# Expert layers that compute each token's own experts only, in four layers of cross-attention and mixture of experts

## The chip, the cores and the metric

The kernel runs on one core of one Trainium2 chip. Its time is the device time of one execution in microseconds. A time of a kernel is the median of its runs; a profile belongs to one execution, whose own time is given beside it. TensorE is called PE (its weight loads PEld), VectorE DVE, ScalarE ACT, GpSimd POOL, SyncE SP.

## The reference

The input x is 8 batches of 128 tokens of 128 channels, in fp32, and there is a context of the same shape. Four layers each add an attention and then a feed-forward of experts:

```python
x = x + L0_xattn(layernorm(x), ctx)     # talking heads
x = x + L0_ffn(layernorm(x))
x = x + L1_xattn(layernorm(x), ...)     # an mLSTM
x = x + L1_ffn(layernorm(x), ...)       # holds one more attention and a layer norm of its own
x = x + L2_xattn(layernorm(x), ...)
x = x + L2_ffn(layernorm(x), ...)
x = x + L3_xattn(ctx, layernorm(x), ...)
x = x + L3_ffn(layernorm(x), ...)
```

In each feed-forward a router gives every token one score for each of 8 experts. Layer 0 takes the best two of 8 experts (hidden width 176, silu gate) with the softmax of the two scores as weights. Layer 1 takes the best one of 8 (width 512, gelu, weight 1). Layer 2 takes the best two of 8 (width 256, silu gate, sigmoid scores divided by their sum) and adds a shared expert. Layer 3 has 7 experts (width 512, silu gate) and 8 router columns; it takes the best one with twice its softmax probability, none where the eighth column wins, and adds a shared expert:

```python
for j in range(NUM_EXPERTS - 1):
    mask = (ind == j)[..., None]
    acc = acc + swiglu(x, Wu[j], Wg[j], Wd[j]) * mask
out = out + ALPHA * p * acc
out = out + swiglu(x, Wu_s, Wg_s, Wd_s)
```

The reference computes every expert on every token and masks. What a token gets is only the output of its own experts.

## The kernel before

The 8 tiles of x (128 tokens by 128 channels) stay in SBUF. Tokens are worked on in two halves of 4 batches, 512 columns each. The stages follow one another, and each engine takes its instructions in a fixed order, which follows the order of the program closely: attention 0 (the L0 talking heads), experts f0, the mLSTM (stage name L1 attention), attention m1 (inside layer 1's feed-forward), experts f1, attention m2, experts f2, attention m3, experts f3.

`layernorm` takes half of the tokens: bn_stats and bn_aggr for each batch on DVE, the power -0.5 for four batches at once on POOL (L108), then z for each batch on DVE. `transposed` turns z into channels by tokens with four PE transposes. `router_logits`, `rank`, `share` and `chosen` give for each half a gate for every token and expert, zero for those not chosen.

`experts` is dense: for each unit (an expert, or in f0 two experts packed together) it loads the weights `w` on SP's queue (L206, four buffers, so loads run ahead), and for each half and each 128 wide chunk of hidden channels computes g (L213) and u (L220) as matmuls of 128x512, silu on ACT (L225) or gelu (L217), and their product on DVE (L226). The down matmuls y (L231) have 128 columns for a batch. DVE adds y times the gate to x (L241, L243).

`attention` (m1, m2, m3) goes over the 8 batches as a software pipeline. In each round DVE takes the negative maxima of the next batch's scores (nmp, L318); `outputs` of the batch before makes the attention's values av (L357), their reciprocal sums rd (L363), cT (L365), the output projection with wo and calls `finish`, which adds to x (`add_to_x` L383, or `to_x1` at L728 and L729); then `weights` transposes the maxima (nt, L330), adds them to q (qm, L332), and makes st and its exponentials pt (L345):

```python
for b in range(B + 1):
    if b + 1 < B:
        q0s[b + 1] = maxima(b + 1, *halves[(b + 1) // HB])
    if b > 0:
        outputs(b - 1, pts.pop(b - 1))
    if b < B:
        pts[b] = weights(b, q0s.pop(b), halves[b // HB][1])
```

PSUM is shared by two tags: `mm` with 6 banks for wide results and `o` with 2 banks. `vz` is a large zeroed tile that POOL fills ahead of the mLSTM (L538). At the end SP stores the 8 tiles of x.

Of the kernel before, what the change touches and what calls it, by code (L numbers as in the profile page):

```python
# [8 lines left out]

FP = mybir.dt.float32  # L10
U8 = mybir.dt.uint8
AF = mybir.ActivationFunctionType
# [20 lines left out]
C_N = 612  # L33
# [16 lines left out]
def blocks(ctx: ExitStack, tc: tile.TileContext, t: dict, out: bass.AP):  # L50
# [3 lines left out]
    act = ctx.enter_context(tc.tile_pool(name="act", bufs=1))  # L54
    small = ctx.enter_context(tc.tile_pool(name="small", bufs=3))
    wpool = ctx.enter_context(tc.tile_pool(name="wpool", bufs=4))
# [24 lines left out]
    ones = keep.tile([1, P], FP, name="ones")  # L81
    nc.gpsimd.memset(ones, 1.0)
# [9 lines left out]
    low = cst[:, C_LOW : C_LOW + 64]  # L92
# [5 lines left out]
    def layernorm(src, name):  # L98
# [10 lines left out]
        z = act.tile([P, HB, P], FP, name=f"z_{name}", tag="z", bufs=3)  # L109
# [20 lines left out]
    def router_logits(zT, wcol, brow, name):  # L130
        lg = bank_o(f"lg_{name}")
        for j in range(HB):
            dst = lg[:, j * E : (j + 1) * E]
            nc.tensor.matmul(
                dst, lhsT=zT[:, j * P : (j + 1) * P], rhs=wsm[:, wcol : wcol + E],
                start=True, stop=brow is None,
            )
            if brow is not None:
                nc.tensor.matmul(
                    dst, lhsT=ones, rhs=row[:, brow : brow + E], start=False, stop=True  # L140
                )
        v = small.tile([P, HB, E], FP, name=f"v_{name}", tag="rt_v")
        nc.vector.tensor_copy(v.rearrange("p b e -> p (b e)"), lg[:, : HB * E])
        return v

    def over_experts(v, op, name, negate=False):
        m = small.tile([P, HB], FP, name=f"m_{name}", tag=f"rt_m{op}")
        nc.vector.tensor_reduce(m, v, AX.X, op, negate=negate)
        return m

    def spread(m):
        return m.unsqueeze(2).to_broadcast([P, HB, E])

    def rank(v, name):

        full = [P, HB, E, E]
        of_j = v.unsqueeze(2).to_broadcast(full)
        of_e = v.unsqueeze(3).to_broadcast(full)
        gt = small.tile(full, FP, name=f"gt_{name}", tag="rt_gt", bufs=2)
        eq = small.tile(full, FP, name=f"eq_{name}", tag="rt_eq", bufs=2)  # L160
        nc.vector.tensor_tensor(gt, of_j, of_e, ALU.is_gt)
        nc.vector.tensor_tensor(eq, of_j, of_e, ALU.is_equal)
        eqf = eq.rearrange("p b e j -> p b (e j)")
        gtf = gt.rearrange("p b e j -> p b (e j)")
        nc.vector.tensor_tensor(
            eqf, eqf, low.unsqueeze(1).to_broadcast([P, HB, E * E]), ALU.mult
        )
        nc.vector.tensor_tensor(gtf, gtf, eqf, ALU.add)
        rk = small.tile([P, HB, E], FP, name=f"rk_{name}", tag="rt_rk")
        nc.vector.tensor_reduce(rk, gt, AX.X, ALU.add)  # L170
        return rk

    def softmax_terms(v, name):
        nm = over_experts(v, ALU.max, f"max_{name}")
        d = small.tile([P, HB, E], FP, name=f"d_{name}", tag="rt_d")
        nc.vector.tensor_tensor(d, v, spread(nm), ALU.subtract)
        e = small.tile([P, HB, E], FP, name=f"e_{name}", tag="rt_e")
        nc.scalar.activation(e, d, AF.Exp)
        return e

    def share(v, name):

        s = over_experts(v, ALU.add, f"sum_{name}")
        r = small.tile([P, HB], FP, name=f"r_{name}", tag="rt_r")
        nc.vector.reciprocal(r, s)
        g = small.tile([P, HB, E], FP, name=f"g_{name}", tag="rt_g")
        nc.vector.tensor_tensor(g, v, spread(r), ALU.mult)
        return g

    def chosen(rk, n, v, name):  # L190
        c = small.tile([P, HB, E], FP, name=f"c_{name}", tag="rt_c")
        if v is None:
            nc.vector.tensor_scalar(c, rk, float(n), None, ALU.is_lt)
        else:
            nc.vector.scalar_tensor_tensor(c, rk, float(n), v, ALU.is_lt, ALU.mult)
        return c

    def experts(name, wdram, cols, zT, gates, func, nchunk, gated, down):

        with tc.tile_pool(name=f"h_{name}", bufs=2) as hidp:
            for u in range(wdram.shape[0]):
                w = wpool.tile([P, cols], FP, name=f"w_{name}_{u}", tag="w")
                nc.sync.dma_start(out=w, in_=wdram[u])  # L206
                up0 = nchunk * P
                dn0 = 2 * nchunk * P if gated else nchunk * P
                for hf in range(NH):
                    hid = hidp.tile([P, nchunk, HT], FP, name=f"hid_{name}_{u}_{hf}", tag="hid")  # L210
                    for c in range(nchunk):
                        g = bank_mm(f"g_{name}_{u}_{hf}_{c}")
                        nc.tensor.matmul(  # L213
                            g, lhsT=w[:, c * P : (c + 1) * P], rhs=zT[hf], start=True, stop=True
                        )
                        if not gated:
                            nc.scalar.activation(hid[:, c, :], g, func)  # L217
                            continue
                        up = bank_mm(f"u_{name}_{u}_{hf}_{c}")
                        nc.tensor.matmul(  # L220
                            up, lhsT=w[:, up0 + c * P : up0 + (c + 1) * P], rhs=zT[hf],
                            start=True, stop=True,
                        )
                        sg = hidp.tile([P, HT], FP, name=f"sg_{name}_{u}_{hf}_{c}", tag="sg", bufs=3)
                        nc.scalar.activation(sg, g, func)  # L225
                        nc.vector.tensor_tensor(hid[:, c, :], up, sg, ALU.mult)  # L226
                    for col, parts in down(u):
                        y = bank_o(f"y_{name}_{u}_{hf}_{col}")
                        for j in range(HB):
                            for n, (c, r0, k) in enumerate(parts):  # L230
                                nc.tensor.matmul(  # L231
                                    y[:, j * P : (j + 1) * P],
                                    lhsT=hid[r0 : r0 + k, c, j * P : (j + 1) * P],
                                    rhs=w[r0 : r0 + k, dn0 + c * P : dn0 + (c + 1) * P],
                                    start=n == 0, stop=n == len(parts) - 1,
                                )
                        for j in range(HB):
                            xb = x[hf * HB + j]
                            yj = y[:, j * P : (j + 1) * P]
                            if col is None:  # L240
                                nc.vector.tensor_tensor(xb, yj, xb, ALU.add)  # L241
                            else:
                                nc.vector.scalar_tensor_tensor(  # L243
                                    xb, yj, gates[hf][:, j, col : col + 1], xb, ALU.mult, ALU.add
                                )
# [144 lines left out]

    with tc.tile_pool(name="a0", bufs=2) as ap:
        w0 = ap.tile([P, 4, 1024], FP, name="w0", bufs=1)
        for i in range(4):
            nc.sync.dma_start(out=w0[:, i, :], in_=t["w0"][:, i, :])
        th = ap.tile([P, 2, 16], FP, name="th", bufs=1)
# [10 lines left out]
        for hf in range(NH):  # L408
# [81 lines left out]
            def outputs(j, pr):  # L490
# [35 lines left out]
                add_to_x(b, o[:, :P])  # L526


            prs = [weights(0)]
            for j in range(HB):  # L530
                if j + 1 < HB:
                    prs.append(weights(j + 1))
                outputs(j, prs[j])

# [13 lines left out]
    )  # L548


    zTs, gates = [], []
    for hf in range(NH):
        zT = transposed(layernorm(half(hf), f"f0_{hf}"), f"f0_{hf}")
        v = router_logits(zT, W_G0, None, f"f0_{hf}")
        rk = rank(v, f"f0_{hf}")
        gates.append(share(chosen(rk, 2, softmax_terms(v, f"f0_{hf}"), f"f0_{hf}"), f"f0_{hf}"))
        zTs.append(zT)
    experts(
        "f0", t["f0"], 9 * P, zTs, gates, AF.Silu, 3, True,
        lambda u: [  # L560
            (2 * u, [(0, 0, P), (2, 0, M0_REST)]),
            (2 * u + 1, [(1, 0, P), (2, 64, M0_REST)]),
        ],
    )


# [153 lines left out]
    for hf in range(NH):  # L720
        z = layernorm(half(hf), f"f1_{hf}")
        z1 = layernorm([z[:, j, :] for j in range(HB)], f"f1i_{hf}")
        zTs.append(transposed(z1, f"f1i_{hf}", W_LN))
        for j in range(HB):
            nc.gpsimd.tensor_copy(x1[hf * HB + j], z[:, j, :])

    def to_x1(b, o):
        nc.vector.tensor_tensor(x1[b], o, x1[b], ALU.add)  # L728
        nc.gpsimd.tensor_tensor(x[b], x[b], x1[b], ALU.add)  # L729
# [188 lines left out]
```

## Time and profile before

| what | value |
|---|---|
| median of 3 runs | 1165.52 us (1152.72, 1165.52, 1170.35) |
| profiled execution | 1148.92 us, span 1147.1 us, mean granted PE clock 0.891 |
| PE busy | 998.9 us (87%) |
| DVE, ACT, POOL busy | 487.6, 312.9, 137.8 us |
| DMA | 23.27 MB, mean 20 GB/s |
| stage attention 0 | 0 to 237 us |
| stages f0; f1; f2; f3 | 237 to 347; 547 to 669; 764 to 866; 960 to 1147 us |
| stages mLSTM; m1; m2; m3 | 347 to 452; 452 to 547; 669 to 764; 866 to 960 us |

The stage bounds are read from the timeline, rounded, so that windows can be cut there. The profile gives for each group of instructions the source line, the engine, the operation, the tiles written and read (out<-in), the shapes, the count, the busy time and the mean duration, then the idle time of the engine ahead of it and what ended most of that idle time. A row of the windows gives start and end, length, busy time and number of instructions for PE, PEld, DVE, ACT and POOL, the granted PE clock, the share of DMA time and GB/s. A row of the timeline gives the start, the time from the first to the last of a run of like instructions, engine, line, operation and tiles, and in brackets an idle time before it with its releaser.

### The profile page before, as it was taken

To read this page: it belongs to the slowest core of one execution; us is meant where nothing else is said; L and a number is where in the kernel's file an instruction comes from. 1 tells how busy PE (TensorE), PEld (TensorE's weight loads), DVE (VectorE), ACT (ScalarE), POOL (GpSimd) and SP (SyncE) were. 2 spreads that over 40 slices of the span, in tenths; PEclk is the share of its full clock that TensorE was granted. 3 is DMA by queue.
4 is the path that set the end of the run, shared out by engine and by line. 5 is a ranking of instruction groups with operands and counts; after the bars stand their busy time and mean duration, and the time that the engine had idled before them with its cause. 6 is when DMAs were issued, how large, how long until landed. Compare 5 with 4: busy or idle time off the path is not lost.

```text
span 1147.1 us, 15509 instructions
## 1 busy us (share of the span) xinstructions
PE 998.9 (87%) x6356; PEld 650.3 (57%) x6356; DVE 487.6 (43%) x1226; ACT 312.9 (27%) x691; POOL 137.8 (12%) x151
## 2 busy tenths in 40 slices
PE   5877977879997992888899988879997887999998
PEld 2456645755556452565677745646664665666665
DVE  3344434443342546564311144644446463433333
ACT  1445345431111111222233311223221222322221
POOL 0112012220002212330000032200004120000000
PEclk9799979989995865889899988989998786999999
DMA  6000000000001000000010000000111000001000
GB/s 246 1 1 1 1 1 1 1 5 19 18 19 37 1 0 0 1 2 1 19 37 33 28 15 1 1 1 29 42 56 55 1 2 1 28 28 35 22 1 19
DMA packets 8892, 23.27 MB, mean 20 GB/s; under 512 B 1010, under 2 KB 4212, under 8 KB 8692
## 3 DMA queue, kind: packets, MB, share of 16 engines
q1 hardware_dynamic: 8098, 20.06, 5.2%
q10 hardware_dynamic: 722, 2.21, 0.5%
q8 instruction: 50, 0.82, 0.3%
q14 instruction: 22, 0.18, 0.1%
HBM read 21.74 MB, written 0.52 MB: 19 GB/s over the span
## 4 chain that ended last, share of the span: by engine, by line
PE 67%; issue 14%; DVE 12%; ACT 3%; POOL 2%; DMA 1%; POOLq 0%; DVEq 0%; SPq 0%; ACTq 0%
PE y_f L231 11%; PE u_f L220 10%; PE g_f L213 10%; DVE nmp L318 4%; PE mx L248 4%; PE st_m L248 3%; PE sc_m L248 3%; PE m L248 2%; PE av_m L357 2%; PE qk L248 2%; PE gb L248 2%; PE av L248 2%; PE st L461 1%; PE kp_m L280 1%; PE o L522 1%
## 5 line engine op out<-in xcount | busy, mean ns | idle before, releaser
L231 PEld LDWEIGHTS y_f<-w_f,hid_f 128*128 128x128 f32 (+1 forms) x1472 | 186.0, 192 | 68.0 <-issue 31.0
L231 PE MATMUL y_f<-w_f,hid_f 128*128 128x128 f32 (+1 forms) x1472 | 202.2, 284 | 1.0 <-DVE hid_f L226 1.0
L225 ACT ACTIVATE sg_f<-g_f 128x512 f32<-128x512 f32 x124 | 74.0, 597 | 262.2 <-PE g_f L213 169.0
L220 PE MATMUL u_f<-zT_f,w_f 128*128 128x512 f32 x248 | 133.2, 620 | 0.0
L213 PE MATMUL g_f<-zT_f,w_f 128*128 128x512 f32 x248 | 133.2, 620 | 0.0
L226 DVE TENSOR_TENSOR hid_f<-u_f,sg_f 128x512 f32<-128x512 f32 x124 | 85.4, 689 | 86.8 <-PE u_f L220 83.3
L345 ACT ACTIVATE pt_m<-st_m 128x512 f32<-128x512 f32 x96 | 50.2, 602 | 168.7 <-PE st_m L248 168.1
L243 DVE SCALAR_TENSOR_TENSOR x<-y_f,c_f,x 128x128 f32<-128x128 f32 x120 | 33.8, 344 | 140.1 <-PE y_f L231 140.1
L248 PE MATMUL st_m<-qm_m,kT_m 32*128 32x256 f32 x384 | 48.1, 470 | 31.7 <-DVE qm_m L332 31.7
L318 DVE TENSOR_REDUCE nmp<-sc_m 128x4 f32<-128x512 f32 x96 | 59.4, 685 | 34.3 <-PE sc_m L248 34.3
L220 PEld LDWEIGHTS u_f<-zT_f,w_f 128*128 128x128 f32 x248 | 45.9, 199 | 44.0 <-issue 43.2
L213 PEld LDWEIGHTS g_f<-zT_f,w_f 128*128 128x128 f32 x248 | 46.0, 201 | 39.7 <-issue 38.9
L248 PE MATMUL mx<-s,kron 128*128 128x512 f32 x64 | 43.8, 772 | 25.1 <-DVE s L469 13.9
L243 DVE SCALAR_TENSOR_TENSOR x<-y_f,g_f,x 128x128 f32<-128x128 f32 x128 | 36.0, 344 | 66.3 <-PE y_f L231 66.3
L213 PE MATMUL g_f<-zT_f1e,w_f 128*128 128x512 f32 x128 | 63.3, 616 | 0.0
L248 PE MATMUL sc_m<-km_m,qT_m 32*128 32x256 f32 x384 | 58.7, 478 | 1.0 <-DVE nmp L318 0.6
L217 ACT ACTIVATE hid_f<-g_f 128x512 f32<-128x512 f32 x64 | 38.2, 597 | 74.2 <-PE g_f L213 74.2
L484 POOL TENSOR_TENSOR pr<-pr,rs 128x512 f32<-128x512 f32 x32 | 33.2, 1039 | 163.6 <-DVE rs L483 134.5
L248 PEld LDWEIGHTS st_m<-qm_m,kT_m 32*128 32x128 f32 x384 | 25.9, 207 | 41.4 <-DVE qm_m L332 37.6
L477 ACT ACTIVATE pr<-mx,nm 128x128 f32<-128x128 f32 x128 | 45.3, 369 | 12.4 <-DVE nm L474 12.4
L248 PEld LDWEIGHTS sc_m<-km_m,qT_m 32*128 32x128 f32 x384 | 40.0, 220 | 14.3 <-ACT pt_m L345 7.0
L108 POOL TENSOR_TENSOR rs_a<-ve_a,nhalf 128x4 f32<-128x4 f32 x8 | 8.1, 1014 | 328.2 <-DVE ve_a L106 328.2
(207 smaller groups left out, 1283.5 us busy)
## 6 DMA issues: line engine op xcount, KB each, us to landing
w_f<-in_f SPq DMA_DIRECT2D x8, 768.0 KB, 4.2
w_f<-in_f SPq DMA_DIRECT2D x8, 512.0 KB, 3.4
w_f<-in_f SPq DMA_DIRECT2D x9, 384.0 KB, 2.9
w_f<-in_f SPq DMA_DIRECT2D x4, 576.0 KB, 8.3
w<-in_w SPq DMA_DIRECT2D x4, 512.0 KB, 8.4
wsm<-in_wsm ACTq DMA_DIRECT2D x1, 1194.0 KB, 7.8
x<-in_x SPq DMA_DIRECT2D x8, 64.0 KB, 3.5
ctxT<-in_ctxT ACTq DMA_DIRECT2D x1, 512.0 KB, 4.5
```

Of the source, the lines that this page charges most:

```text
L213: nc.tensor.matmul(g, lhsT=w[:, c * P : (c + 1) * P], rhs=zT[hf], start=True, stop=True)
L217: nc.scalar.activation(hid[:, c, :], g, func)
L220: nc.tensor.matmul(up, lhsT=w[:, up0 + c * P : up0 + (c + 1) * P], rhs=zT[hf], start=True, stop=True,)
L225: nc.scalar.activation(sg, g, func)
L226: nc.vector.tensor_tensor(hid[:, c, :], up, sg, ALU.mult)
L231: nc.tensor.matmul(y[:, j * P : (j + 1) * P], lhsT=hid[r0 : r0 + k, c, j * P : (j + 1) * P], rhs=w[r0 : r0 + k, dn0 + c * P : dn0 + (c + 1 ...
L243: nc.vector.scalar_tensor_tensor(xb, yj, gates[hf][:, j, col : col + 1], xb, ALU.mult, ALU.add)
L248: nc.tensor.matmul(dst, lhsT=w, rhs=src, start=True, stop=True)
L318: nc.vector.tensor_reduce(nmp[:, :, r * 32 + 8 : r * 32 + 153 : 144], sc[r].rearrange("p (c h k) -> p c h k", c=2, h=2), AX.X, ALU.max, ne ...
L345: nc.scalar.activation(pt[:, r].rearrange("p c h q -> p (c h q)"), st[r], AF.Exp)
L477: nc.scalar.activation(pr[:, gg, :], m3[:, g, :], AF.Exp, bias=nm[:, g : g + 1], accum_out=sums[:, gg : gg + 1],)
L484: nc.gpsimd.tensor_tensor(pr[:, part, :], pr[:, part, :], rs.unsqueeze(2).to_broadcast([P, 4, P]), ALU.mult,)
```

## The change

The dense loops are gone. Each expert layer is now an object of the class `Routed` with these steps.

- `route(b, src)` is called once for each batch, from the attention's `finish`: a layer norm of one batch (with the power on POOL), one PE transpose, logits, the best values and their indices (DVE max and max_index), one-hot rows, and a matmul with a triangle of ones that counts at which position of its expert's region each token stands; then POOL scatters the rows of z, once for each chosen expert, to `routed_z` in DRAM by an indirect DMA. A region holds 1024 rows for each expert.
- `run` computes a fixed number of blocks of 128 rows. The first 128 rows of each expert are the static groups, up to four experts together; their weights are loaded ahead (`static_weights`, tag ws). After them `table` makes, on PE and DVE, a list of what further blocks there are. Up to 15 (f0, f2) or 7 (f1, f3) further blocks come in groups of four: SP reads a word of the table into a register and uses it as the address of the weight load and of the row load; the results are stored on SP at the same address in `routed_y`. The weight buffers for these are 8 in f0 and 4 in f1 to f3.
- `combine` gathers each token's results from `routed_y` by an indirect DMA on POOL and adds them to x with the gate.

The shared experts of f2 and f3 are dense as before (`shared`). Blocks computed are the same number whatever the tokens chose. At the start SP fills `routed_z` and `routed_y` with zeros (10240 rows of 512 bytes each). SP issues 197 transfers in place of 51, reads 44 words into registers, and POOL issues 96 indirect transfers. In f0 each expert has weights of its own, 320 KB, where two shared a unit of 576 KB.

The core of the diff:

```diff
+        def route(self, b, src):
+            z = layernorm1(src, name)
+            pb = bank_o(f"rt_{name}")
+            nc.tensor.transpose(pb[:, :P], z, ident)
+            zT = self.zT[:, b * P : (b + 1) * P]
...
+            nc.tensor.matmul(lg, lhsT=zT, rhs=wsm[:, self.wcol : self.wcol + E], ...)
...
+                nc.vector.tensor_copy(v, lg)
+            nc.vector.max(out=vm, in_=v)
+            nc.vector.max_index(out=ix, in_max=vm, in_values=v)
+            nc.vector.tensor_tensor(oh, ..., iota8..., ALU.is_equal)
...
+            nc.tensor.matmul(pos, lhsT=tri, rhs=c, start=True, stop=False)
+            nc.tensor.matmul(pos, lhsT=ones128, rhs=self.sums, start=False, stop=True)
+            nc.vector.tensor_tensor(sums, self.sums, c, ALU.add)
+            nc.vector.tensor_tensor(sel, oh, pos..., ALU.mult)
+                nc.vector.tensor_reduce(self.idx[:, b, :], sel, AX.X, ALU.add)
+            for k in range(top):
+                nc.gpsimd.indirect_dma_start(
+                    out=self.views[b * top + k],
+                    out_offset=bass.IndirectOffsetOnAxis(ap=self.idx[:, b, k : k + 1], axis=0),
+                    in_=z, in_offset=None,
+                )
...
+                for q in range(2):
...
+                    load = nc.sync.dma_start(out=zq[:, :m, :], in_=by_expert(routed_z)[:, es, :])
+                    yq = blocks_of(zq, static[es], m, f"{name}_{q}")
+                    nc.scalar.dma_start(out=by_expert(yv[q])[:, es, :], in_=yq[:, :m, :])
+                tab = self.table()
+                for i0 in range(0, n, 4):
...
+                            r = nc.values_load(tab[0:1, i : i + 1], engines=[mybir.EngineType.SP], ...)
+                            nc.sync.dma_start(
+                                out=w, in_=wdram[bass.ds(r // B, 1)].rearrange("o p c -> p (o c)")
+                            )
+                            nc.sync.dma_start(
+                                out=zq[:, i - i0, :],
+                                in_=by_block(routed_z)[bass.ds(r, 1)].rearrange("o p c -> p (o c)"),
+                            )
...
+                    yq = blocks_of(zq, ws, m, f"{name}_d{i0}")
+                    for i in range(m):
+                        nc.sync.dma_start(out=by_block(yv[2 + i0 + i])[bass.ds(at[i], 1)]..., in_=yq[:, i, :])
...
+        def combine(self, b, gates):
+            for k in range(self.top):
+                nc.gpsimd.indirect_dma_start(
+                    out=yk, out_offset=None, in_=routed_y,
+                    in_offset=bass.IndirectOffsetOnAxis(ap=self.idx[:, b, k : k + 1], axis=0),
+                )
+                    nc.vector.scalar_tensor_tensor(
+                        x[b], yk, gates[:, b, k : k + 1], x[b], ALU.mult, ALU.add
+                    )
...
+        for dram in (routed_z, routed_y):
+            nc.sync.dma_start(
+                out=dram.rearrange("(p n) c -> p n c", n=BLOCKS),
+                in_=zero.unsqueeze(1).to_broadcast([P, BLOCKS, P]),
+            )
...
                 add_to_x(b, o[:, :P])
+                f0.route(b, x[b])
...
+    wst = ctx.enter_context(tc.tile_pool(name="wst", bufs=9))
+    wdyn = ctx.enter_context(tc.tile_pool(name="wdyn", bufs=4))
+    ws1 = static_weights(wst, "f1", t["f1"], 8 * P, 0, E)
...
     def to_x1(b, o):
         nc.vector.tensor_tensor(x1[b], o, x1[b], ALU.add)
         nc.gpsimd.tensor_tensor(x[b], x[b], x1[b], ALU.add)
+        f1.route(b, x1[b])
...
-    experts(
-        "f1", t["f1"], 8 * P, zTs, gates, AF.Gelu_apprx_tanh, 4, False,
-        lambda u: [(u, every4)],
-    )
+    f1.run(t["f1"], 8 * P, ws1, hidden_plain, parts_of(4, 4), wdyn)
+    for b in range(B):
+        f1.combine(b, None)
...
+    shared("f2s", ws2[E], f2.zT, 2)
+    f2.run(t["f2"], 6 * P, ws2[:E], hidden_gated(2), parts_of(2, 4), wdyn)
```

`blocks_of` transposes the four blocks of rows into one PSUM bank (PE), copies them to SBUF (DVE), computes the hidden part (`hidden0`, `hidden_plain` or `hidden_gated`: PE matmuls of 128 columns, the activation on ACT over up to 512 columns, the product on DVE), the down matmuls into one bank, and copies the results out on ACT.

More of the change, by code (lines that the diff above doesn't have):

```diff
@@ L190, in chosen @@
[L190 to L210, printed above, removed]
+            v = self.v[:, b, :]
```

491 lines of the change are left out of this document (336 added, 155 removed).

## The prediction

> **What bounds the kernel now.** I read, in this order: the page's engine rows and clock, the chain that ended last, the groups of the expert loops, the table of windows by stage, and the timeline of one batch of an attention.
>
> ```profile
> span 1147.1 us, 15509 instructions
> PE 998.9 (87%) x6356; PEld 650.3 (57%) x6356; DVE 487.6 (43%) x1226; ACT 312.9 (27%) x691; POOL 137.8 (12%) x151
> ...
> PE 67%; issue 14%; DVE 12%; ACT 3%; POOL 2%; DMA 1%; POOLq 0%; DVEq 0%; SPq 0%; ACTq 0%
> ...
> L231 PE MATMUL y_f<-w_f,hid_f 128*128 128x128 f32 (+1 forms) x1472 | 202.2, 284 | 1.0 <-DVE hid_f L226 1.0
> ...
> L220 PE MATMUL u_f<-zT_f,w_f 128*128 128x512 f32 x248 | 133.2, 620 | 0.0
> ```
>
> PE is busy 87% and two thirds of the last chain: the kernel as a whole is PE-bound. But it has two kinds of stages. Windows (length, then busy time of PE, PEld, DVE, ACT, POOL with counts, granted clock, DMA share, GB/s), here layer 0's experts, attention 1, experts 1, experts 2, experts 3:
>
> ```profile
> 237.00:347.00 110.00, 102.72 (x375) 59.33 (x374) 45.63 (x131) 19.22 (x30) 7.51 (x6) 0.90 0.05 16
> ...
> 452.00:547.00 95.00, 74.89 (x874) 51.97 (x872) 52.75 (x120) 20.54 (x37) 24.35 (x32) 0.84 0.01 1
> 547.00:669.00 122.00, 119.67 (x664) 86.71 (x664) 24.70 (x89) 39.62 (x66) 3.68 (x6) 0.96 0.08 28
> ...
> 764.00:866.00 102.00, 98.53 (x446) 61.47 (x447) 47.61 (x133) 25.79 (x41) 1.16 (x1) 0.97 0.13 43
> ...
> 960.00:1147.10 187.10, 178.61 (x864) 113.11 (x858) 69.72 (x164) 45.78 (x75) 1.01 (x1) 0.97 0.06 20
> ```
>
> Expert stages are PE and nothing else (clock 0.90 to 0.97). The attentions are not: a batch there is a round of waits, 7.8 us from one nmp to the next (514.99 to 522.76):
>
> ```profile
> 514.99 2.48 DVE L318 TENSOR_REDUCE nmp<-sc_m 128x4 f32<-128x512 f32 x4 [0.32 <-PE sc_m L248]
> 517.44 0.96 DVE L363 RECIPROCAL rd_m<-av_m 128x128 f32<-128x128 f32 x1
> 518.31 0.63 DVE L332 TENSOR_TENSOR qm_m<-nt_m,q_m 128x512 f32<-128x512 f32 x1
> 518.86 0.28 DVE L365 TENSOR_TENSOR cT_m<-av_m,rd_m 128x128 f32<-128x128 f32 x1
> 519.00 0.69 PE L248 MATMUL st_m<-qm_m,kT_m 32*128 32x256 f32 x2 [1.04 <-DVE qm_m L332]
> 520.14 0.29 DVE L728 TENSOR_TENSOR x<-av_m,x 128x128 f32<-128x128 f32 x1 [1.01 <-PE av_m L248]
> 522.76 2.48 DVE L318 TENSOR_REDUCE nmp<-sc_m 128x4 f32<-128x512 f32 x4 [1.78 <-PE sc_m L248]
> ```
>
> DVE and PE hand to each other; what is put between cT and qm is paid in full.
>
> **PE work removed.** A 128x512 matmul takes 0.86 us at full clock (two records of 0.43), a 128-column one 0.22. Dense, the four expert layers cost 93, 112, 95 and 167 us of it (467). After, 23, 15, 23 and 14 blocks of 128 rows and two shared experts cost 36, 28, 44 and 60 (168). So 300 us of PE work go. They are not 300 us of time, since a stage now is a row of steps that wait for each other.
>
> **Added to the attentions.** The finish of each batch now routes it before the next batch's weights step: on DVE behind the x addition stand bn_stats, aggr, ve and z, and z waits for POOL's power; only then qm. From the timeline: cT moves up to 518.4, wo (0.76 later before) to 519.2, x to 519.7; from x to z in the half layer norm took 2.2 (bn 0.33, aggr 0.33, ve 0.25, POOL 1.01, hops), z 0.34: 522.2. On PE the transpose of z stands ahead of nt: 0.35 and 0.66 and a hop, so qm starts at 523.5, not 518.31: +5.2. Then the position matmul stands among the st matmuls and waits for copy, max, index and one-hot on DVE behind qm, four at 0.17 to 0.34: +0.3. That is 5.5 for 7 batches in 3 attentions: **+115** (bounds 4.3 and 7.1 each: 90, 150). Behind the waiting qm stand st, the exponentials, sc and the next nmp, so nothing covers it.
>
> Attention 0 gets the same, but its PE has other work to overlap, and POOL's pr (1.04 us, L484) stands behind the scatters: 2.6 for 7 batches, **+18** (8 to 30). The zero fill, 10.5 MB, takes 43 us at the 246 GB/s of the first slice, beside the early projections; the first scatter comes after the first x addition at 78.7. I cost it at nothing; at half that rate POOL stands some 30 us.
>
> **The expert stages, from the last x addition (T) on.** Not shown in the trace: an indirect DMA's issue on POOL (between SP's own issue, 0.33, and POOL's longest operation, a memset of 4.36; I take POOL's power, 1.0, a small POOL instruction), its landing (1.6 to 4.2, from these rows; I take 2.5), and the read of a table word into an SP register (between a semaphore step, 0.02, and a landing, 3.5; I take an issue, 0.33, the nearest SP work). With two DMA issues and address steps a block costs SP 1.5 (0.7 to 4.7).
>
> ```profile
> w_f<-in_f SPq DMA_DIRECT2D x8, 768.0 KB, 4.2
> ...
> w_f<-in_f SPq DMA_DIRECT2D x9, 384.0 KB, 2.9
> ...
> x<-in_x SPq DMA_DIRECT2D x8, 64.0 KB, 3.5
> ...
> out_x<-x SPq DMA_DIRECT2D x8, 64.0 KB, 1.6
> ```
>
> - Lead: route 6.2, scatter 1.0 and 2.5, load 0.3 and 2.5: 12.5 (one more scatter for two experts).
> - A group of four blocks, alone on PE: transposes 0.5 to 1.2, copy 0.69, matmuls 2.6 to 7 for the hidden part, silu 0.60, product 0.69, downs 1.6 to 7, copy out 0.60, six hops of 0.25: 10 (f0, f2), 13 (f1), 14 (f3).
> - Table: one matmul and nine small DVE operations, 3. It stands behind the static groups, and the first weight address needs it: loads then take 4 x 1.5 + 3 = 9.
> - In f1 to f3 there are four weight buffers, so a next group's loads wait for this one's downs: copy 0.9, stores and loads on the same queue, landing: 11.5 ahead of each next group. f0 has eight, and this is hidden.
> - Tail: store 4 to 5, gathers 1.0 each and 2.5.
>
> f0: 13.5 + 2x10 + 3 + 9 + 4x10 + 4 + 4.4 (POOL's memset of vz among the gathers) + 16 + 2.5 = 112; before 110 (237.3 to 347.6): +2. f1, to the next layer norm's first half: 12.5 + 26 + 3 + 9 + 13 + 11 + 10 + 4 + 6.5 = 95; before 117 (545.4 to 662.3): -22. f2: the shared expert covers the lead and ends at 23, + 20 + 3 + 9 + 10 + 3 x 21.5 + 5 + 10.5 = 145; before 100.5: +44. f3: 40 + 24.5 + 3 + 9 + 14 + 11.5 + 11 + 4 + 11.5 + 1.5 = 130; before 178.7 (968.4 to the end): -49. Together **-25**.
>
> **Sum**: 1147 + 115 + 18 - 25 = 1255 span, 1257 as an execution (2 us lie around the span). The shown median, 1165.5, lies 1.4% above its profiled execution (1148.9); I leave that to the range. About 2% is what a measurement of this kernel can tell from no change, 23 us.
>
> The Trainium skill ("DMA: Bandwidth & Descriptors", Latency and other measured facts) gives a register read a floor of some 600 ns; no run here shows it yet. By it the 33 reads on the path would add some 9 us to the sum. The same page (Anatomy of one DMA, SWDGE (gpsimd) path) puts a fixed cost of about 2.0 us on every DMA, which speaks against a change that makes 51 transfers on SP into 197 and adds 96 on POOL. The 64 KB rows above, 1.6 and 3.5 us, hold such a cost.
>
> **Rivals.**
> *The groups run back to back (faster).* If SP runs ahead and PE stays the bound inside a group, the 20 groups (6, 4, 6 and 4) cost their matmuls at full clock, 168 less 52 of the shared experts, 116, and not 60 + 52 + 60 + 49 = 221; the five waits of 11.5 shrink to a landing of 2.5. That saves 105 + 45 = 150: span 1105, 1107 as an execution. It decides once it saves some 115. For: loads land in 3 to 4 us beside 10 us of compute. Against: four buffers, a table behind the static groups, and the hops. Chance 0.17.
> *The routing hides (no change).* If only the stretch to z is paid, 2.2 for 21 batches is 46: 1186, 1188. For: DVE is busy 53 of 95 us in attention 1. Against: qm stands behind z. Chance 0.13.
> *The run-time parts are dear (slower still).* A register read at 2.4 adds 2.1 for 33 blocks, 70; gathers at 2 us add 36: 1361, 1363. For: nothing of the kind is in the trace. Against: SP's own steps there are under 0.6. Chance 0.2.
> Mine has 0.5. Faster 0.17, same 0.13, slower 0.70. The bounds together reach from 1147 + 90 + 8 - 175 = 1070 to over 1400; 8 in 10 lie between 1150 and 1350.
>
> **What would show it.** Right: nmp to nmp near 13 us in attentions 1 to 3, qm waiting on PE behind z; PE busy some 300 us less; f3 near 130 and f2 near 145; in f2 PE idle some 11 us between groups with a DMA as releaser. Wrong: nmp to nmp under 10, or expert stages under 90 us each; SP steps of a block under 1 us; gathers that pass POOL at 0.3.

## The result, and the profile after

The changed kernel takes 1297.91 us (median of 4 runs, 1284.85 to 1299.92), the kernel before on the same chip 1160.02 us. The ratio is 1.119, with a 95% interval of 1.1065 to 1.1312: slower by 12%. The profiled execution has a span of 1295.8 us. Its page begins so (lines left out are marked); the last four lines are engine shares of the chain that ended last and three of the groups by line (busy, mean ns, idle before and its releaser):

```profile
span 1295.8 us, 14530 instructions
...
PE 880.5 (68%) x5601; PEld 629.0 (49%) x5601; DVE 446.4 (34%) x1234; ACT 255.0 (20%) x616; POOL 243.6 (19%) x272
...
PEclk9867878787655765766667676666866576568976
...
PE 57%; DVE 14%; issue 9%; DMA 9%; POOL 4%; ACT 4%; SPq 3%; POOLq 0%; ACTq 0%; DVEq 0%
...
L358 POOL DMA_INDIRECT yk_f<-routed_y,idx_f x48 | 46.2, 962 | 356.7 <-DMA routed_y<-yq_f_d 190.8
...
L242 POOL DMA_INDIRECT routed_z<-z_f,idx_f x48 | 49.2, 1025 | 134.9 <-DVE idx_f L240 130.0
L292 PE MATMUL zp_f_d<-cst,zd_f 128*128 128x128 f32 x44 | 18.2, 436 | 81.4 <-DMA zd_f<-routed_z 81.4
```

PE is busy 118 us less, not 300: the mean granted clock fell from 0.891 to 0.697, so that what is left takes longer. PE waits 81.4 us for row blocks, DMA has gone from 1% to 9% of the last chain, and the row PEclk is mostly at 5 to 7 tenths from the eleventh slice on. The windows by stage (columns as before) are those of f0, m1, f1, f2 and f3:

```profile
280.00:400.00 120.00, 61.06 (x266) 48.03 (x266) 26.80 (x79) 12.07 (x21) 25.38 (x25) 0.62 0.28 82
...
518.00:651.00 133.00, 102.34 (x907) 73.86 (x905) 57.88 (x154) 23.07 (x43) 30.92 (x37) 0.65 0.01 4
651.00:735.00 84.00, 42.40 (x266) 38.73 (x266) 9.01 (x33) 12.83 (x21) 6.74 (x8) 0.68 0.34 109
...
900.00:1025.00 125.00, 65.27 (x351) 55.15 (x350) 24.45 (x68) 16.45 (x27) 11.11 (x12) 0.70 0.41 127
...
1181.00:1295.80 114.80, 67.19 (x452) 57.46 (x450) 26.40 (x69) 19.43 (x31) 9.20 (x10) 0.80 0.23 74
```

Over the stages of the table below, PE's busy time in the four expert stages fell from 488 to 237 us (f3: 171.4 to 66.9). Attention m1, with 907 matmul records where it had 874, took 102 us of PE where it took 75, at a clock of 0.65 where it had 0.84.

To add up, the span is cut at the last x addition of each attention and at the point where each expert layer hands on: for f0 the end of its last addition to x, for f1 and f2 the start of the next layer norm's fourth bn_stats. The same cuts are used for every experiment below (us, from each run's profiled execution):

| run | att. 0 | f0 | mLSTM + m1 | f1 | m2 | f2 | m3 | f3 | span |
|---|---|---|---|---|---|---|---|---|---|
| before | 237.0 | 110.6 | 197.5 | 118.0 | 103.2 | 102.5 | 99.3 | 179.0 | 1147.1 |
| after | 280.0 | 120.5 | 250.1 | 85.4 | 163.3 | 126.1 | 155.8 | 114.5 | 1295.8 |
| e1 route later | 269.7 | 113.8 | 231.6 | 84.8 | 142.5 | 121.7 | 132.8 | 116.6 | 1213.6 |
| e2 warm | 271.1 | 113.8 | 248.1 | 86.6 | 169.1 | 127.5 | 148.8 | 115.0 | 1280.0 |
| e3 routing alone | 276.7 | 115.2 | 250.0 | 125.6 | 166.3 | 112.2 | 145.4 | 187.8 | 1379.2 |
| e4 all buffers | 277.5 | 116.0 | 262.8 | 75.8 | 169.4 | 99.0 | 155.7 | 105.0 | 1261.2 |
| e5 route behind | 229.3 | 143.5 | 204.2 | 91.7 | 103.3 | 120.8 | 108.8 | 118.5 | 1120.1 |
| e6 hold scatters | 271.5 | 116.8 | 252.9 | 85.4 | 163.3 | 124.5 | 154.0 | 114.8 | 1283.2 |
| e7 fixed blocks | 281.2 | 97.1 | 248.9 | 58.5 | 164.7 | 77.9 | 156.4 | 86.1 | 1170.6 |
| layers 1 and 3 only | 234.5 | 112.9 | 205.5 | 92.1 | 106.0 | 102.5 | 90.6 | 121.9 | 1066.1 |
| layer 3 only | 229.2 | 113.1 | 218.3 | 118.0 | 103.2 | 102.9 | 91.4 | 124.6 | 1100.6 |
| layer 3 only, again | 234.0 | 113.0 | 205.6 | 118.4 | 113.2 | 104.8 | 99.0 | 122.5 | 1110.6 |

The last two rows also show how much a stage varies whose code is that of before: the mLSTM with m1 took 197.5 to 218.3 us, m2 103.2 to 113.2. The profiled execution of before (1148.92 us) is besides a little faster than the four runs behind its median (1152.72 to 1170.35).

From before to after the four attention columns grow by 43, 53, 60 and 57, in all 212 us; the expert columns change by +10, -33, +24 and -65, in all -64. That is the 149 us of the result.

One batch of m1 shows where an attention's time goes. This is the timeline of the changed kernel (start, length, then engine, line, operation, and the idle time before):

```profile
598.39 2.48 DVE L547 TENSOR_REDUCE nmp<-sc_m 128x4 f32<-128x512 f32 x4 [3.29 <-PE sc_m L477]
...
599.12 1.94 PE L586 MATMUL av_m<-pt_m,vz 128*32 128x128 f32 x32
...
600.83 1.73 PE L586 MATMUL av_m<-pt_m,cst 128*32 128x128 f32 x32
602.63 0.96 DVE L592 RECIPROCAL rd_m<-av_m 128x128 f32<-128x128 f32 x1 [1.75 <-PE av_m L586]
603.62 0.29 DVE L594 TENSOR_TENSOR cT_m<-av_m,rd_m 128x128 f32<-128x128 f32 x1
...
604.49 0.29 DVE L976 TENSOR_TENSOR x<-av_m,x 128x128 f32<-128x128 f32 x1 [0.58 <-PE av_m L477]
...
606.20 0.35 DVE L160 TENSOR_SCALAR z_f<-x,mv_f,rs_f 128x128 f32<-128x128 f32 x1 [0.68 <-POOL rs_f L158]
...
606.60 0.48 PE L193 MATMUL rt_f<-cst,z_f 128*128 128x128 f32 x1 [2.14 <-DVE z_f L160]
...
607.97 0.69 DVE L561 TENSOR_TENSOR qm_m<-nt_m,q_m 128x512 f32<-128x512 f32 x1 [1.42 <-PE nt_m L559]
...
608.71 1.22 PE L477 MATMUL st_m<-qm_m,kT_m 32*128 32x256 f32 x4
...
609.92 0.59 PE L232 MATMUL rt_f<-oh_f,cst 128*128 128x8 f32 x2
...
614.62 2.48 DVE L547 TENSOR_REDUCE nmp<-sc_m 128x4 f32<-128x512 f32 x4 [3.29 <-PE sc_m L477]
```

From nmp to nmp it is 16.23 us; it was 7.77. Step by step, after against before: nmp to rd 4.24 and 2.45, rd to qm 5.34 and 0.87, qm to st 0.74 and 0.69, st to the next nmp 5.91 and 3.76. The second is the routing itself: x, statistics, POOL's power, z, and PE's transpose stand between rd and qm. In the fourth, PE does the position matmuls in the middle of st, 0.95 us (609.92 to 610.87). The rest, 1.8 and 1.2, is mostly the same matmuls at a lower clock: the two groups of av take 1.94 and 1.73 where, before, they took 1.08 and 1.06:

```profile
515.42 1.08 PE L357 MATMUL av_m<-pt_m,vz 128*32 128x128 f32 x32
...
516.31 1.06 PE L357 MATMUL av_m<-pt_m,cst 128*32 128x128 f32 x32
```

This pair of rounds shows more than the average one: 7.77 us was among the shortest rounds before. From the first qm to the last in m1, m2 and m3, 21 rounds, it was 196.5 us before and is 352.4: from 9.4 to 16.8 a round, 7.4 more. The rounds before differ with the clock. Two of m1, qm to qm, with the same 102 PE records (columns as above, the clock third from the end):

```profile
518.30:526.00 7.70, 6.62 (x102) 4.76 (x102) 4.84 (x11) 2.06 (x4) 1.49 (x2) 1.00 0.01 2
491.40:501.80 10.40, 9.58 (x102) 7.10 (x102) 5.06 (x12) 2.06 (x4) 2.54 (x3) 0.67 0.00 0
```

A busy share of PE therefore says little by itself: the slower matmuls of a low clock fill it, 92% in the second round and 86% in the first.

### The profile page after: what moved, and what is told of

It reads as the page before. It is cut to its first block, busy times and chain, and to the rows that moved or that the text cites. A ratio compares the mean times of both kernels' runs of the same rounds, so it can differ in the third digit from the quotient of the medians.

```text
span 1295.8 us, 14530 instructions
## 1 busy us (share of the span) xinstructions
PE 880.5 (68%) x5601; PEld 629.0 (49%) x5601; DVE 446.4 (34%) x1234; ACT 255.0 (20%) x616; POOL 243.6 (19%) x272
## 4 chain that ended last, share of the span: by engine, by line
PE 57%; DVE 14%; issue 9%; DMA 9%; POOL 4%; ACT 4%; SPq 3%; POOLq 0%; ACTq 0%; DVEq 0%
PE av_m L586 5%; PE st_m L477 4%; PE mx L477 4%; PE sc_m L477 3%; PE g_f_d L477 3%; DMA yk_f<-routed_y,idx_f 3%; DMA zd_f<-routed_z 3%; PE y_f_d L307 2%; PE g_f L477 2%; PE qk L477 2%; PE st L700 2%; PE u_f_d L477 2%; PE y_f L307 2%; PE gb L477 2%; DVE nmp L547 2%
## 5 line engine op out<-in xcount | busy, mean ns | idle before, releaser
L358 POOL DMA_INDIRECT yk_f<-routed_y,idx_f x48 | 46.2, 962 | 356.7 <-DMA routed_y<-yq_f_d 190.8
L477 PE MATMUL st_m<-qm_m,kT_m 32*128 32x256 f32 x384 | 73.7, 667 | 11.1 <-DVE qm_m L561 10.9
L242 POOL DMA_INDIRECT routed_z<-z_f,idx_f x48 | 49.2, 1025 | 134.9 <-DVE idx_f L240 130.0
L292 PE MATMUL zp_f_d<-cst,zd_f 128*128 128x128 f32 x44 | 18.2, 436 | 81.4 <-DMA zd_f<-routed_z 81.4
L477 PE MATMUL g_f_d<-zq_f_d,wd_f 128*128 128x128 f32 x202 | 47.6, 394 | 9.2 <-DVE zq_f_d L295 5.2
L477 PEld LDWEIGHTS g_f_d<-zq_f_d,wd_f 128*128 128x128 f32 x202 | 42.3, 299 | 13.0 <-DVE zq_f_d L295 7.3
L158 POOL TENSOR_TENSOR rs_f<-ve_f,nhalf 128x1 f32<-128x1 f32 x32 | 18.1, 566 | 160.6 <-DVE ve_f L156 158.5
L586 PE MATMUL av_m<-pt_m,vz 128*32 128x128 f32 x768 | 47.0, 399 | 1.3 <-ACT pt_m L574 1.3
L592 DVE RECIPROCAL rd_m<-av_m 128x128 f32<-128x128 f32 x24 | 22.9, 956 | 61.7 <-PE av_m L586 61.7
L586 PEld LDWEIGHTS av_m<-pt_m,vz 128*32 128x32 f32 x768 | 32.5, 160 | 23.1 <-issue 14.1
## 6 DMA issues: line engine op xcount, KB each, us to landing
routed_z<-zero SPq DMA_DIRECT2D x1, 5120.0 KB, 21.7
routed_y<-zero SPq DMA_DIRECT2D x1, 5120.0 KB, 38.8
```

Source lines behind the costliest of these rows:

```text
L242: nc.gpsimd.indirect_dma_start(out=self.views[b * top + k], out_offset=bass.IndirectOffsetOnAxis(ap=self.idx[:, b, k : k + 1], axis=0), in ...
L292: nc.tensor.transpose(tp[:, i * P : (i + 1) * P], zq[:, i, :], ident)
L358: nc.gpsimd.indirect_dma_start(out=yk, out_offset=None, in_=routed_y, in_offset=bass.IndirectOffsetOnAxis(ap=self.idx[:, b, k : k + 1], ax ...
L477: nc.tensor.matmul(dst, lhsT=w, rhs=src, start=True, stop=True)
L586: nc.tensor.matmul(av[j * 32 : j * 32 + 32, part * P : (part + 1) * P], lhsT=w, rhs=pt[:, h % 8 // 2, h // 8, h % 2, :], start=i == 0, sto ...
L592: nc.vector.reciprocal(rd, av[:, P : 2 * P])
```

## The experiments

The theory after this reading (W in the expectations): routing in the attentions' chain is the cost, and PE, idle in those waits, is also given a lower clock. The main rival (C): the clock is low because the expert stages no longer keep PE busy. Others are named with the runs.

**e3, routing alone.** The kernel before, dense experts and all, with `route` called from each attention's finish and the scatters as in the change; nothing reads what they write:

```diff
                 add_to_x(b, o[:, :P])
+                f0r.route(b, x[b])
...
         nc.gpsimd.tensor_tensor(x[b], x[b], x1[b], ALU.add)
+        f1r.route(b, x1[b])
...
```

> The kernel before with the per-batch routing and the scatters added to its four attentions as the change has them; nothing reads what is scattered, the dense experts stay, so this is the cost of that part alone. Theory W: the waits and the clock that falls with them are the attentions' own, so the costs seen in the changed kernel appear whole: attention 0 +43, m1 +50, m2 +55, m3 +52, about 1350 us. Rival C (attentions are slow because the expert stages ahead of them leave PE cold): only the chain, 43 and 3 times 38, about 1305 us or less. The prediction's own prices (18 and 115) would give 1282.

It took 1380.99 us. The attentions cost +40, +53, +63 and +46 here, where the expert stages were dense and had clocks of 0.87 to 0.95. m1's clock was 0.62:

```profile
509.00:642.00 133.00, 102.50 (x904) 74.18 (x902) 57.21 (x153) 22.29 (x42) 30.88 (x37) 0.62 0.01 4
642.00:768.00 126.00, 121.13 (x657) 88.04 (x658) 29.99 (x124) 39.24 (x65) 4.11 (x5) 0.94 0.08 27
```

So rival C is out as the main cause: the fall is the attention's own, and dense stages ahead of it do not prevent it. (The total is 30 us above what was expected, since the expert stages grew by 5 to 10 us each: from the attention's last x to the first addition of an expert it takes 5 to 10 us longer, with the last batch's routing in front of the experts' own.)

**e2, PE kept busy.** Five matmuls of 256 columns on x are put ahead of the transpose of z in m1 to m3:

```diff
             pb = bank_o(f"rt_{name}")
+            for i in range(self.warm):
+                project(pb[:, 256:512], src, wsm[:, 0:256])
             nc.tensor.transpose(pb[:, :P], z, ident)
```

> The changed kernel with five extra matmuls of 128x256 per batch in m1, m2 and m3, on the batch's x into an unused part of the routing's bank, just ahead of the transpose of z, where PE waits for about 2.1 us. At full clock they take 2.2 us, at half 4.3. If the clock follows how busy PE is within the stage: the clock of m1 to m3 rises from 0.64 to 0.72 or more, and the batch period stays within 0.5 us of 16 or falls, in spite of the work added. If the clock has another cause: it stays at 0.64, and the period grows by 1 to 2 us, 20 to 45 us in all.

It took 1281.77 us, once; the changed kernel's runs begin at 1284.85. The windows of m1 and of two of its rounds, qm to qm (the clock is third from the end):

```profile
503.00:633.00 130.00, 107.62 (x977) 77.89 (x975) 57.69 (x154) 22.96 (x43) 30.93 (x37) 0.79 0.01 5
...
543.00:555.80 12.80, 10.02 (x121) 7.52 (x121) 7.00 (x20) 2.51 (x6) 4.16 (x5) 1.00 0.02 6
572.80:589.80 17.00, 14.66 (x121) 10.90 (x121) 7.13 (x20) 2.52 (x5) 3.11 (x4) 0.70 0.02 5
```

The clock went from 0.65 to 0.79 in m1, from 0.63 to 0.69 in m2 and to 0.77 in m3. The mLSTM, m1, m2 and m3 together were 566 us against 569, with 24 batches of added matmuls in them. So the clock depends on what PE does in the stage; in m2 it stayed below the 0.72 that was expected. The two rounds show what it is worth: with the same 121 PE records, routing and added matmuls included, a round takes 12.8 us at full clock and 17.0 at 0.70, where the changed kernel's takes 16.2. Most rounds stayed at the low clock, so as a remedy it gives nothing: the added work eats what the clock returns.

**e1, the routing later in the attention.** In m1 to m3, layer norm to one-hot stand behind the next batch's weights step, the position and the scatter behind the maxima after that:

```diff
                     q0s[b + 1] = maxima(b + 1, *halves[(b + 1) // HB])
+                if b > 1:
+                    later[0].route_at(b - 2)
...
                     pts[b] = weights(b, q0s.pop(b), halves[b // HB][1])
+                if b > 0:
+                    later[0].route_z(b - 1, later[1][b - 1])
+                    later[0].route_v(b - 1)
```

> In attentions m1, m2 and m3 the routing of a batch is issued behind the next batch's weights step, in two parts (layer norm to one-hot behind weights, position and scatter behind the next maxima). The computation is the same. Theory W (the routing's place between cT and qm makes the wait, and the idle PE then lowers its own clock): nmp to nmp falls from about 16 us to 9 to 10, the clock in these stages rises from 0.64 to about 0.8, and 21 batches give about 140 us back: about 1158 us. Rival C (the clock is low because the expert stages no longer keep PE busy, whatever the attention does): the place gives back only the 5.5 us per batch of the chain, 115 us, and the clock stays near 0.65: about 1183 us. Rival D (DVE and PE work of the routing itself is what costs, wherever it stands): under 50 us come back, over 1245 us.

1229.23 us (1215.37 to 1236.33), a ratio of 1.059 (1.0513 to 1.0666): 62 us came back in the three stages (profiled executions), not the 140 that W expected nor the 115 of C. The time lies between C and D, and none of the three had it. The period fell from 16.2 to 13.6, not to 9. The timeline of DVE shows why (e1, m1):

```profile
560.73 0.96 DVE L608 RECIPROCAL rd_m<-av_m 128x128 f32<-128x128 f32 x1 [2.24 <-PE av_m L602]
561.61 0.63 DVE L577 TENSOR_TENSOR qm_m<-nt_m,q_m 128x512 f32<-128x512 f32 x1
...
565.15 0.35 DVE L160 TENSOR_SCALAR z_f<-x,mv_f,rs_f 128x128 f32<-128x128 f32 x1 [0.68 <-POOL rs_f L158]
568.40 0.17 DVE L226 COPY v_f<-rt_f 128x8 f32<-128x8 f32 x1 [2.90 <-PE rt_f L217]
...
569.28 0.17 DVE L251 TENSOR_TENSOR cs_f<-cs_f,oh_f 128x8 f32<-128x8 f32 x1
569.39 1.29 DVE L563 TENSOR_REDUCE nmp<-sc_m 128x4 f32<-128x512 f32 x2
```

qm now stands right behind rd. But DVE waits 2.90 us for the router's logits, and six small operations and that wait stand ahead of the next nmp; on PE, the transpose of z and the logits stand among sc and wait for POOL and ACT. The hand-overs were moved within the round, not out of it, and the clock stayed at 0.66 to 0.68.

**e6, the scatters of attention 0.** The prediction put attention 0's cost on POOL, where pr stands behind the scatters. Here they wait until the half's last pr:

```diff
+            with tc.issue_after(last["pool"].ins):
+                for j in range(HB):
+                    f0.scatter(hf * HB + j)
```

> The changed kernel with one edit: attention 0's scatters are held back on POOL until the last pr of the half has been scaled; routing up to the index stays where it is, inside the attention. Attention 0 took 277 to 280 us in the changed kernel's runs that had its routing so, 237 before and 229 with routing behind it. If the prediction's reason for attention 0 holds (POOL's pr stands behind the scatters, 2.2 to 2.6 us a batch): 15 us or more come back, 262 us or less. If the waits of PE and DVE for the routing's steps make it: less than 8 us come back, 270 or more.

Attention 0 took 271.5 us. The same attention 0, scatters in place, took between 269.7 and 281.2 in five other runs of the table, so nothing came back that can be told from its own spread. The scatters are not the cause.

**e4, more buffers for the further blocks.** f1 and f2 get a buffer for every further block (7 and 15); f3, which has 7 further blocks, gets six. Of the edit, the old pool and f2's new one:

```diff
-    wdyn = ctx.enter_context(tc.tile_pool(name="wdyn", bufs=4))
...
+    with tc.tile_pool(name="wdf2", bufs=15, reuse_waits="tile") as wdyn:
+        f2.run(t["f2"], 6 * P, ws2[:E], hidden_gated(2), parts_of(2, 4), wdyn)
...
```

> The changed kernel with a weight buffer for every further block (7 in f1, 15 in f2, 6 in f3) in place of four. If the wait of a next group's loads for the downs of this one sets the group period in f2 (20.2 us from transpose to transpose now): the period falls to 12 to 14, f2 gives back 18 to 24 us, f1 and f3 5 to 9 each, in all 30 to 40: about 1262 us. If SP's own time for a block (1.9 us between row loads) or the eight transfers in flight set it: under 12 us come back.

1262.93 us: f1, f2 and f3 gave back 10, 27 and 10. That is 46 where 30 to 40 were expected; that the total met 1262 is luck, since the mLSTM with m1, and m2, whose code is the same, were 13 and 6 us longer in this run. In f2 PE's transposes of the first three further groups began so in the changed kernel, and those of the first two so in e4:

```profile
938.51 0.48 PE L292 MATMUL zp_f_d<-cst,zd_f 128*128 128x128 f32 x1 [5.61 <-DMA zd_f<-routed_z]
...
955.55 0.33 PE L292 MATMUL zp_f_d<-cst,zd_f 128*128 128x128 f32 x1 [1.55 <-DMA zd_f<-routed_z]
960.37 0.48 PE L292 MATMUL zp_f_d<-cst,zd_f 128*128 128x128 f32 x1 [4.50 <-DMA zd_f<-routed_z]
...
976.21 0.30 PE L292 MATMUL zp_f_d<-cst,zd_f 128*128 128x128 f32 x1 [1.89 <-DMA zd_f<-routed_z]
```

```profile
941.01 0.47 PE L292 MATMUL zp_f_d<-cst,zd_f 128*128 128x128 f32 x1 [5.85 <-DMA zd_f<-routed_z]
...
954.16 0.27 PE L292 MATMUL zp_f_d<-cst,zd_f 128*128 128x128 f32 x1
955.39 0.49 PE L292 MATMUL zp_f_d<-cst,zd_f 128*128 128x128 f32 x3
```

With four buffers the second group's rows come in over nine microseconds; with fifteen they are there. The group periods went from 17.0, 20.7 and 20.0 us to 13.2, 8.5 and 15.2, and PE's wait for the further blocks' rows in f2 from 35.0 to 14.7. The wait for the last group's downs was the main limit, as the prediction had it.

**e7, places fixed beforehand.** On top of e4, a further block's place is a constant; table and register reads are gone:

```diff
-                            r = nc.values_load(tab[0:1, i : i + 1], ...)
+                            r = (i % ne) * B + 1 + i // ne
```

> The kernel with all buffers (1263 us), but the further blocks stand at places fixed beforehand (the second block of each expert, then the third), so there is no table, no register read and no wait of a weight's address for the static groups; as many blocks, loads and stores. Tokens that lie elsewhere are left out. If the run-time address costs its wait, from the static groups' end to the first further transpose (8 to 12 us a layer now, and 1.3 to 1.9 us between a group's row loads): f1, f2 and f3 each give 10 to 15 us back and f0 10, about 1215 to 1225 us. If transfers and POOL's gathers set the stages all the same: under 15 us, over 1248.

1172.41 us. f0, f1, f2 and f3 gave back 19, 17, 21 and 19 against e4, 76 in all, more than the 40 to 55 expected: with a fixed address the weights need not wait for anything of their layer, and rows follow right behind the scatters. (Another 14 us lie in the mLSTM and m1, which vary by as much between the runs whose code is the same there, 248.9 to 262.8.) So finding the further blocks at run time, with table, reads, and loads that cannot start ahead, costs about 19 us a layer; the run does not separate these.

**e5, the routing behind the attention.** All four layers are still routed, with e4's buffers in f1 to f3. Layer norm and logits are made for half of the tokens at once; best experts, positions and scatters are not issued before the attention's last x:

```diff
+            for hf in range(NH):
+                self.route_half(hf, src[hf * HB : (hf + 1) * HB])
+            with tc.issue_after(dve.ins), tc.issue_after(pe.ins):
+                for hf in range(NH):
+                    self.place(hf)
```

> All four layers stay routed, with a weight buffer for every further block as in the run before (7, 15 and 6). Layer norm and logits are made for half of the tokens at once, as in the kernel before, and best experts, positions and scatters are held back until the attention's last x is added. Theory W (the attentions were slow only because routing stood in their chain): attention 0 is 237 us again, nmp to nmp about 8, clock there above 0.8; the expert stages take 77, 98 and 105 us as with all buffers, plus 5 to 15 for the routing that is now in front of them, and 120 plus 15 for f0: about 1100 us, 4 to 6% faster than before. Rival C (the expert stages, no longer dense, leave PE cold for the attention that follows): the mLSTM, m2 and m3 stay 10 to 20 us longer each, 1130 to 1150. Rival D (routing costs as much behind the attention as inside it): over 1200.

1128.99 us (1121.88 to 1143.16), a ratio of 0.97 (0.9629 to 0.977): faster than before by 3%. The period in m1 is 7.72 us again, qm to qm:

```profile
527.21 0.63 DVE L603 TENSOR_TENSOR qm_m<-nt_m,q_m 128x512 f32<-128x512 f32 x1
...
531.66 2.48 DVE L589 TENSOR_REDUCE nmp<-sc_m 128x4 f32<-128x512 f32 x4 [1.78 <-PE sc_m L519]
...
534.93 0.63 DVE L603 TENSOR_TENSOR qm_m<-nt_m,q_m 128x512 f32<-128x512 f32 x1
```

The four attention columns are 646 us in sum, before 637, after 849. The routing now costs where it stands: against e4, f0 +28, f1 +16, f2 +22, f3 +14, more than the 5 to 15 that were expected, and so the total is 1129 and not 1100. The mLSTM with m1, and m3, are 7 and 10 us longer than before, each behind a routed expert stage. For the first that does not speak for rival C: behind a dense f0 it took 205.5, 218.3 and 205.6 us in the last three rows of the table, against 204.2 here. m3 took 90.6 to 99.3 us behind a dense f2 and 108.8 here; there a part of rival C may be left, which one execution does not show.

**Only the layers where it pays.** By e5's columns f1 and f3 gain 26 and 61 us, f0 and f2 lose 33 and 18. So the kernel before was given, in one version, layer 3 routed and, in another, layers 1 and 3, both as in e5, with four weight buffers in f3.

> The kernel before with only layer 3's experts routed, routing held back behind m3's last x as in the run above; four weight buffers for the further blocks. f3's stage was 179 us dense and 114 routed (105 with six buffers); its shared expert, 35 us of matmuls, covers routing and scatters. Theory W: nothing changes ahead of T3, the stage is 110 to 118 us, in all 1080 to 1090 as an execution. If routing cannot hide behind the shared expert: 15 to 25 us more.

> As the run above, with layer 1's experts routed too (a buffer for each of the 7 further blocks). f1's stage was 118 us dense and 77 routed with all buffers; it has no shared expert, so 10 to 15 us of routing come in front. Theory W: 25 to 30 us less than with layer 3 alone, about 1055. Rival C: m2 behind the now cold f1 loses 10 to 20 us of that.

> The kernel with only layer 3 routed, behind m3, once more, for a ratio: its runs lay between 1085.67 and 1116.29. Expected 1080 to 1095, a ratio of 0.93 to 0.945, and so 15 to 25 us above the kernel with layers 1 and 3 routed.

Layer 3 alone: 1085.67 to 1116.29 us the first time, and 1112.29 (1100.68 to 1115.69) the second, a ratio of 0.955 (0.9468 to 0.9637); 1080 to 1095 was expected. Its f3 took 123 to 125 us, more than the 110 to 118 expected, and the stages ahead of it, whose code is that of before, took 976 and 988 us where the profile of before has 968. Layers 1 and 3: 1069.92 us (1065.23 to 1073.11), a ratio of 0.921 (0.9164 to 0.9253). That is the fastest version, 8% faster than before and 18% under the changed kernel's median (1069.92 to 1297.91). It is 42 us under layer 3 alone, where 25 to 30 were expected, though 15 above the 1055 that was named. Its windows of f1 and m2 show that m2 behind a routed f1 still has a clock of 0.80; it is 3 us longer than before, within what m2 takes behind a dense f1 (103.2 to 113.2), so rival C's 10 to 20 us did not come:

```profile
553.00:646.00 93.00, 49.27 (x309) 45.93 (x309) 15.34 (x87) 12.37 (x20) 15.27 (x16) 0.67 0.40 138
646.00:751.00 105.00, 85.62 (x884) 54.95 (x884) 49.79 (x110) 22.64 (x41) 24.99 (x29) 0.80 0.01 3
```

## Why the prediction was right, and where it was off

The sign and the reason held: the span was forecast at 1255 and was 1295.8, inside 1150 to 1350, and the added waits in the attentions outweighed what the experts gained. That the span came within 41 us is in part luck: the attentions were forecast at +133 and grew by 212, the expert stages at -25 and changed by -64, and the two errors offset each other. Of the signs named, qm waits on PE behind z, and in f2 PE waits for rows between groups. But PE's busy time fell by 118 us and not by 300, rounds are 16.2 us and not 13, and f2 and f3 took 126 and 115 us and not 145 and 130. Point by point:

- *The chain in m1 to m3, 5.5 us for 21 batches, 115.* The chain itself is right in sum: rd to qm grew by 4.5, where qm was to start 5.2 later, and the position matmuls hold PE for 0.95, where 0.3 was forecast; 5.4 together. e5, which takes it out, has rounds of 7.72 us again, and e2's rounds at full clock take 12.8, near the 13 that were forecast. What was left out is the clock. The 21 rounds grew by 156 us, 7.4 each; less the chain, 5.4, there remain 2.0 a round, some 42 us, put down to the clock, for which the sum should have had a term. The step that failed is the one that took its durations from a round of before at full clock (7.7 us at 1.00; at 0.67 the same round took 10.4) for a stage that would wait more. The bound above, 150, was just passed.
- *Attention 0, +18 (8 to 30).* Measured 33 to 44. The reason given, pr behind the scatters on POOL, is wrong by e6. e5, 229.3 us with the routing behind, shows that routing's place makes all of it. In the trace PE's last s matmuls stood behind the transpose of z, and DVE's copy of sT waited for them; the position matmuls stood between mx and st; and mx then took 2.08 us where it took 1.12. How much is wait and how much clock was not separated.
- *Zero fill at nothing.* Right: its two transfers were issued at 17.7 and 18.5 us and landed 21.7 and 38.8 us later; the first scatter was issued at 87. e3, which has no zero fill, has nearly the same attention 0 (276.7 against 280.0), and e5 has the fill and 229.3.
- *The expert stages, -25.* Measured -64; f1, f2 and f3 were shorter than forecast by 10 to 19 us, f0 longer by 8. The prices taken were close: POOL's indirect transfer 1.0, landing 2.5, a register read 0.33. Measured (register read on SP, min/median/max in ns; then DMA issues with us to landing):

```profile
L330 SPq TENSOR_LOAD <-tab_f x44: 263/270/1006, 310.9 to 1255.7; - x44
```

```profile
zd_f<-routed_z SPq DMA_DIRECT2D x44, 64.0 KB, 3.5
...
routed_z<-z_f,idx_f POOLq DMA_INDIRECT x48, 2.3
yk_f<-routed_y,idx_f POOLq DMA_INDIRECT x48, 2.5
```

  f2's group period was forecast at 21.5 and is 17.0, 20.7 and 20.0 (first transpose to first transpose); 11.5 us of it as a wait for buffers was not far off, by e4 it is 9 (27 us for three rounds). The group's own cost was set too high: the transposes do start with the first block's rows (938.51, the fourth block's at 944.67), which the sum did not count on; no run separates what else was too high.
- *The rival "the groups run back to back".* e7 comes near to it: the four stages take 320 us where the changed kernel took 447 and the dense one 510. It is what known places, with e4's buffers, would be worth.
- *The rival "the run-time parts are dear".* Not by their instructions, which cost 0.27 and 1.0 us. But finding the blocks at run time, table behind static groups, is 76 us by e7, where the sum had 12 for each of four layers, 48.
- *The rival "the routing hides".* Out: it needed 2.2 us a round, and the rounds grew by 7.4.

The Trainium skill ("DMA: Bandwidth & Descriptors", Latency and other measured facts) has some 600 ns for a register read, by which the 33 reads of the prediction would be an estimated 20 us in all; the median here is 270 ns, and they are worth 9. The prediction also saw a fixed 2.0 us in its 64 KB rows; the 1.6 us of the stores among them lies below that. On the clock it says ("TensorE: Matmul & The Clock Gate", Part 1) that a hardware monitor gates PE's clock by its recent activity. The trace agrees in direction: e2, with one of m1's waits filled, has 0.79 where the changed kernel has 0.65.

## What to carry to other kernels

Before work is hung on each step of a chain in which engines hand to each other, see what stands between one hand-over and the next: here some 5 us of small hand-overs a batch, and the clock lost with them, cost 212 us in four attentions, where 251 us less of PE's busy time in the expert stages gave 64 back. Price such a wait twice, once as time and once as the clock that PE may lose with it, and look at the clock of the round whose durations are used. And weigh each layer alone: sparse work paid where the dense stage was long and something covered the routing (layer 3) or few further blocks were needed (layer 1), and not where there were 15 further blocks whose places are found at run time (f0 and f2: 97 and 78 us with fixed places in e7, dense 111 and 103).

## What the hardware showed that was not expected

The granted clock of m1 fell from 0.84 to 0.65 although PE's single waits in a round were only 2.1 and 1.4 us long. (PE was busy 77% of that stage, as against 79% before, but the slower matmuls fill that share.) Five matmuls in one of these waits brought it to 0.79. The length of the waits alone does not decide it: e1's rounds have waits of 1.0 and 0.8 us and its m1 a clock of 0.68, while e2's round at full clock has a wait of 1.5 us in it. What decides it, these runs leave open. The same round takes 7.7 us at full clock and 10.4 at 0.67. The mLSTM stage, 77% busy and at 0.65 already before, is of the same kind. An indirect DMA of 128 rows of 512 bytes holds POOL for 0.96 us as a gather and 1.03 as a scatter on average, and lands 2.5 and 2.3 us after its issue.
